# Moving the stores of a block-matching denoiser's two layers to later points of the issue order

## The chip, the cores and the metric

The kernel runs on 1 core of one Trainium2 chip. The metric is the time of one execution on the device in microseconds (us): before the change 6535.1 us, the median of three runs (6530.16 to 6537.6). A core has five engines that run side by side: TensorE (PE, with the loading of weights shown apart as PEld), VectorE (DVE), ScalarE (ACT), GpSimd (POOL) and SyncE (SP). Here POOL and SP issue nearly all DMA transfers, and each of them issues in order: an issue that must wait holds up everything behind it on its queue.

## The reference

`x` has 8 images of 32 channels and 128 x 128 pixels, in float32. Both layers begin with a group normalisation (16 groups of two channels) and end with a residual addition:

```
# layer 0: block matching, then a chain of convolutions
xn   = gn(x)
# for each pixel: the 8 of 25 offsets in a 5x5 window whose 3x3 patches differ least
xb   = the 8 shifted copies of xn -> 256 channels
dct  = grouped 1x1 (xb)
h    = relu(dw3x3(1x1(xb)));  h = relu(dw3x3(1x1(h)))
wien = sigmoid(dw3x3(1x1(h)))
x    = x + 1x1(grouped 1x1 (wien * dct))
# layer 1: one 5x5 filter, the same for all channels
x    = x + conv5x5(gn(x), pad=2)
```

## The kernel before, in words

**Slots.** An image is cut into 16 strips of 8 rows. The main loop has one step `s` for each strip, and one more per image (17 in all, `NS + 1`), and every step has four slots: `i = 3, 2, 1` for the three pairs of 1x1 and depthwise 3x3 convolution, each on a strip one step older than the last, and `i = 0` for the last product with `dct`. Half of the 256 channels go through the depthwise convolution on PE (`depthwise_t`, L751), the other half on VectorE (`depthwise_v`: one pass on ACT at L722, then eight of VectorE at L725 on a tile `tv`, then ACT at L729). Two rows of `tv` are carried to the next strip by a copy on SP's queue (`rows_before_v`, L655); the tiles `t` of PE's half are spread over the partitions by copies on SP's queue (L707, L709) and their last rows are carried by L648.

**Gathering.** Each slot also makes a quarter of the next strips' `xb`: POOL loads the index bytes (`gather_load`: `ib` at L602, three buffers, and pixels `xt` at L591), ACT makes selection masks from `ib` (L616, L617), and PE multiplies (L631). The search for the next image's offsets (`prep`, `squares` at L444, `costs`, whose sums are loaded into `dsum` at L492 and L499 and added on VectorE at L508 to L520, then the eight best of 25 at L536 and L537) is dealt out over the steps in small pieces.

**The residual.** `final_add` is a generator. For each strip PE makes the last 1x1 (`pa`, L831), and a resumption later VectorE adds it to the rows of `x` in `xr` (L839), takes their statistics (L840), and POOL stores the sum to the DRAM tile `x1d` in four transfers (L844). In the main loop `later` holds this generator. It is resumed twice in slot `i = 3`: ahead of the slot's product, and after `tick`.

**Layer 1.** After an image's last strip `layer1(b)` is pushed. It treats the channels eight at a time. For each such chunk (`c` = 0, 8, 16, 24) POOL loads `x1d` (L885 to L890), VectorE normalises (L897), PE makes the 5x5 filter as 40 matmuls with banded weights (L924), VectorE adds (L936), and POOL stores to `out` in four transfers (L938). The tiles `xy` and `xm` have two buffers each, and a chunk takes both. Rows 62 to 65 are not in those stores; `middle` makes them on VectorE with 25 passes (L972) and stores them at L981. Layer 1 of image b runs beside layer 0 of image b + 1; that of the last image runs alone at the end, with other buffers (`ends`, `xo`), all its chunks loaded at once, and the next chunk normalised ahead of the additions.

**The order.** Work that has no fixed place is a generator that yields the name of a queue ("D" for VectorE's pieces with a cost, "B", "A", "P", "Q") and optionally a number of turns to wait. `tick` (once per slot) or `turn` counts `now` up, runs pieces of "D" up to a credit and then "B"; the main loop runs "P", "Q" and "A" at fixed places of the slot, "A" after `tick`. PE, DVE and ACT keep the order in which the program issues (`ORDERED`, `manual_schedule`). POOL and SP are not among them: a planner sets their order by when it expects each transfer to be ready.

Of the kernel before, what the change touches and what calls it, by code (L numbers as in the profile page):

```python
# [44 lines left out]
def bm3d_conv_preact(  # L45
# [16 lines left out]
    nc = tc.nc  # L62
# [757 lines left out]
    def final_add(b, n, acc, xr, j0, j1):  # L820

        ya = R * n - 3 + j0
        whole = j1 - j0 == R
        nr, nw = (2, W) if whole else (j1 - j0, C)
        pa = ps_x.tile([P, 512], F32, name=f"pa_{b}_{n}", tag="x")
        pa = pa[:, : nr * nw].rearrange("p (r w) -> p r w", w=nw)
        for m in range(2):
            for j in range(4):
                ra = 2 * j if whole else j0
                xa = 0 if whole else C * j  # L830
                nc.tensor.matmul(  # L831
                    pa[C * j : C * (j + 1)],
                    lagg[:, m],
                    acc[m][:, ra : ra + nr, xa : xa + nw],
                    start=m == 0,
                    stop=m == 1,
                )
        yield
        nc.vector.tensor_add(xr, xr, pa)  # L839
        nc.vector.bn_stats(stats[b][:, n], xr)  # L840
        for j in range(4):
            ra = ya + 2 * j if whole else ya
            xa = 0 if whole else C * j
            nc.gpsimd.dma_start(  # L844
                x1d[b][:, ra : ra + nr, xa : xa + nw], xr[C * j : C * (j + 1)]
            )

    def layer1(b):

        yield "D", 0.2  # L850
        mv = work.tile([P, 2], F32, name=f"mv1_{b}", tag="mv1")
        nc.vector.bn_aggr(mv, stats[b].rearrange("p a b -> p (a b)"))
        mr = yield from group_stats(mv, f"b{b}")
        dg = work.tile([C, 2, C], F32, name=f"dg_{b}", tag="dg")
        for i in range(2):
            nc.vector.tensor_scalar(
                dg[:, i], ident[:C, :C], mr[:C, i : i + 1], None, op0=ALU.mult
            )
        yield "P", 0
        pb = ps_x.tile([P, 512], F32, name=f"pb_{b}", tag="x")  # L860
        nc.tensor.matmul(
            pb[:, : 2 * C], ones, dg.rearrange("p a b -> p (a b)"), start=True, stop=True
        )
        bc = work.tile([P, 2, C], F32, name=f"bc_{b}", tag="bc")
        nc.scalar.copy(bc.rearrange("p a b -> p (a b)"), pb[:, : 2 * C])
        last = b == NB - 1
        if last:
            ends = xnp.tile([P, HR, HX], F32, name="ends", tag="xn")
            ends = ends.rearrange("p r x -> p (r x)")[:, : 8 * 4 * W]
            ends = ends.rearrange("p (g c x) -> p g c x", g=8, x=W)  # L870
        xys = {}

        def load(c):


            if last:
                m = work.tile([P, 2, 4, W], F32, name=f"xo_{c}", tag="sel", bufs=4)
                t = [ends[:, c // 4], ends[:, c // 4 + 1], m[:, 0], m[:, 1]]
            else:
                t = [  # L880
                    work.tile([P, 4, W], F32, name=f"{name}_{b}_{c}_{e}", tag=name)
                    for name, e in (("xy", 0), ("xm", 0), ("xy", 1), ("xm", 1))
                ]
            src = x1d[b].rearrange("c y x -> y c x")
            nc.gpsimd.dma_start(t[0], src[:, c : c + 4])  # L885
            for h in range(2):
                nc.gpsimd.dma_start(
                    t[1][64 * h : 64 * h + 64], src[64 - 64 * h : P - 64 * h, c + 4 : c + 8]
                )
            nc.gpsimd.dma_start(t[2], src[:, c + 4 : c + 8])  # L890
            xys[c] = t

        def normalise(c):
            t = xys[c]
            for e in range(2):
                for i in range(4):
                    nc.vector.tensor_scalar(  # L897
                        t[3 - 2 * e][:, i],
                        t[e][:, i],
                        bc[:, 0, c + 4 * e + i : c + 4 * e + i + 1],  # L900
                        bc[:, 1, c + 4 * e + i : c + 4 * e + i + 1],
                        op0=ALU.subtract,
                        op1=ALU.mult,
                    )

        for c in range(0, C if last else 8, 8):
            load(c)
        push(middle(b, mr))
        for c in range(0, C, 8):
            if c == 0 or not last:  # L910
                yield "D", 2.0, 1 if last else 3
                normalise(c)
            yield "P", 0
            ps = [
                ps_x.tile([P, 4, W], F32, name=f"p5_{b}_{c}_{e}", tag="x") for e in range(2)
            ]
            t = xys.pop(c)

            for k, dx in enumerate((0, -2, -1, 1, 2)):
                xa, xz = max(0, -dx), min(W, W - dx)  # L920
                for h in range(2):
                    for e in range(2):
                        r, o = 64 * h, 64 * ((h + e) % 2)
                        nc.tensor.matmul(  # L924
                            ps[e][o : o + 64, :, xa:xz],
                            band[r : r + 64, dx + 2, r : r + 64],
                            t[3 - 2 * e][r : r + 64, :, xa + dx : xz + dx],
                            start=k == 0,
                            stop=k == 4,
                        )  # L930
            yield "D" if last else "B", 3.6 if last else 1.6
            if last and c + 8 < C:
                normalise(c + 8)
            for e in range(2):
                y = t[2 * e]
                nc.vector.tensor_add(y, y, ps[e])  # L936
                for a, z in ((0, 62), (66, P)):
                    nc.gpsimd.dma_start(  # L938
                        out[b, c + 4 * e : c + 4 * e + 4, a:z].rearrange("c y x -> y c x"),
                        y[a:z],  # L940
                    )
            if c + 8 < C and not last:
                yield "A", 0, 1
                load(c + 8)

        done.add((b, 0))
# [89 lines left out]
    with tc.manual_schedule(engines=ORDERED):  # L1036
# [17 lines left out]
        later = iter(())  # L1054

        for s in range(len(steps) + 2):
# [10 lines left out]
            for i in (3, 2, 1, 0):  # L1067
                si = s - (i - 1 if i else 2)
                live = 0 <= si < len(steps)
                new_v = new_t = iter(())  # L1070
                if live:
                    bi, ni = steps[si]

                if live and i:
                    src = source(i, bi, ni)
                    pointwise_v(i, bi, ni, lws[i - 1], src)
                    new_v, new_t = depthwise_v(i, bi, ni), depthwise_t(i, bi, ni)
                    accs[i, bi, ni] = [None, next(new_v)]
                next(later, None)
                if live and not i:  # L1080
                    if ni == 0:
                        x1d[bi] = dram.tile([C, H, W], F32, name=f"x1d_{bi}", tag="x1d")
                        stats[bi] = work.tile([P, NS + 1, 6], F32, name=f"stat_{bi}", tag="stat")
                    xr, xf, j0, j1 = fins.pop(si)
                run("P")
                if live and not i:
                    final_dct(bi, ni, accs[3, bi, ni], xf, j0, j1)

                run("Q")
                if s < len(steps):  # L1090
                    unit(gather_select, u + 1, (0,))
                    unit(gather_load, u + 3)
                    tick(b, i)
                next(later, None)
                next(new_v, None)
                if live and i:
                    pointwise_t(i, bi, ni, lws[i - 1], src)
                next(kept, None)
                if s < len(steps):
                    unit(gather_pixels, u)  # L1100
                next(dt, None)
                run("A")
                next(dv, None)
                if s < len(steps):
                    unit(gather_select, u + 1, (1,))
                    u += 1
                next(dt, None)
                kept, dv, dt = dv, new_v, new_t
                if live and not i:
                    later = end(bi, ni, xr, j0, j1)  # L1110
                if not i and 0 <= s - 1 < len(steps):
                    fins[s - 1] = final_load(*steps[s - 1])
# [66 lines left out]
```

## Time and profile before

| | |
|---|---|
| median of three runs | 6535.1 us |
| profiled execution, as timed | 6526.97 us |
| its span, first to last instruction | 6525.2 us |
| PE busy | 6180.3 us, 95% |
| DVE busy | 5856.5 us, 90% |
| ACT busy | 5051.0 us, 77% |
| POOL busy | 3077.3 us, 47% |
| granted TensorE clock, mean | 0.979 |
| an output store of layer 1 (L938, 124 KB), issue to landing | median 10.6 us |

The profile is one execution. A timeline line gives start and duration in us, engine, source line, operation, what is written from what, how many instructions are merged, and in brackets the idle time of the engine before it with what ended that. A line of the waits gives who waited, for whom, the us in total, the number of waits and the longest. "L725" is line 725 of the kernel. A wait is put down to what ended last by the profile.

### The profile page before, as it was taken

Reading aid. Unit: us, or ns where it says so; the run is one execution under the profiler, and the core shown is the slowest. Engines: PE = TensorE matmul, PEld = TensorE weight load, DVE = VectorE, ACT = ScalarE, POOL = GpSimd, SP = SyncE. Lnnn points to the kernel's source line nnn. Section 1 sums busy time; section 2 is a strip of 40 time slices with the busy share of each in tenths; the row PEclk is TensorE's granted clock in tenths of the full one; section 3 lists DMA queues with packets and bytes.
Section 4 is the critical chain, followed back from the end, with each engine's and each line's share of the span. In section 5 each row is a group of like instructions: output and inputs, shape, how many; then the busy total and the mean of one; then the engine's idle time right before and its main releaser. Section 6 shows DMA issues by size and latency. Waiting matters only on the chain.

```text
span 6525.2 us, 234180 instructions
## 1 busy us (share of the span) xinstructions
PE 6180.3 (95%) x102306; PEld 3262.3 (50%) x102306; DVE 5856.5 (90%) x8828; ACT 5051.0 (77%) x6698; POOL 3077.3 (47%) x5015
## 2 busy tenths in 40 slices
PE   5799999999999999999999999999999999999997
PEld 1445445544555546454555544544545454465553
DVE  7899988999889998899998999899998999988776
ACT  5787769778787877877778787887869787787772
POOL 8345436444364444643446534454345644344334
PEclk7899999999999999999999999999999999999998
DMA  4555555565555655655546556565555665455553
GB/s 85 125 135 144 123 124 146 145 143 135 133 145 139 142 147 127 150 140 135 141 129 157 140 131 151 127 150 137 139 134 138 150 147 133 118 149 147 137 135 79
DMA packets 544960, 886.21 MB, mean 136 GB/s; under 512 B 248880, under 2 KB 312944, under 8 KB 543936
## 3 DMA queue, kind: packets, MB, share of 16 engines
q0 software_dynamic: 383648, 611.87, 37.4%
q1 hardware_dynamic: 157776, 258.11, 16.4%
q8 instruction: 805, 13.19, 0.9%
q10 hardware_dynamic: 2512, 1.25, 0.1%
q14 instruction: 219, 1.79, 0.1%
HBM read 420.60 MB, written 216.49 MB: 98 GB/s over the span
## 4 chain that ended last, share of the span: by engine, by line
PE 50%; DVE 32%; ACT 5%; POOL 5%; DMA 4%; issue 4%; SPq 0%; ACTq 0%; DVEq 0%; POOLq 0%
DVE acc L725 21%; PE pw L751 16%; PE pv L670 12%; PE p L694 11%; PE pg L631 4%; DVE idx L537 3%; POOL xtd L424 3%; PE pc L810 2%; DVE df L444 2%; DVE acc L818 1%; PE p L924 1%; DVE mx L536 1%; PE pd L459 1%; DMA t<-t 1%; ACT sel L616 1%
## 5 line engine op out<-in xcount | busy, mean ns | idle before, releaser
L725 DVE SCALAR_TENSOR_TENSOR acc<-tv,dwv,acc 128x1024 f32<-128x1024 f32 (+3 forms) x3264 | 4031.6, 1237 | 156.3 <-ACT acc L722 52.0
L751 PE MATMUL pw<-t,dwd 96*32 96x254 f32 (+7 forms) x31680 | 2118.1, 419 | 23.0 <-DMA t<-t 10.1
L751 PEld LDWEIGHTS pw<-t,dwd 96*32 96x32 f32 (+1 forms) x31680 | 1105.7, 110 | 826.8 <-issue 369.3
L616 ACT ACTIVATE sel<-ib,nplace 128x1024 f32<-128x1024 uint8 x1024 | 1170.8, 1143 | 62.0 <-DMA ib<-idxd 62.0
L617 ACT ACTIVATE sel<-sel 128x1024 f32<-128x1024 f32 x1024 | 1086.0, 1061 | 32.5
L670 PE MATMUL pv<-acc,lw 128*32 128x512 f32 x8448 | 959.8, 590 | 54.4 <-DVE acc L818 47.8
L694 PE MATMUL p<-acc,lw 128*32 128x256 f32 x16768 | 974.3, 379 | 2.2 <-issue 2.2
L602 POOL DMA_DIRECT2D ib<-idxd x512 | 292.0, 570 | 1207.3 <-ACT sel L616 1078.1
L791 POOL DMA_DIRECT2D xf<-xbd x1088 | 651.0, 632 | 279.9 <-PE pc L810 180.6
L694 PEld LDWEIGHTS p<-acc,lw 128*32 128x32 f32 x16768 | 570.7, 111 | 393.6 <-issue 67.4
L729 ACT ACTIVATE acc<-acc 128x1024 f32<-128x1024 f32 (+3 forms) x408 | 417.1, 1022 | 390.2 <-DVE acc L725 389.8
L678 ACT COPY tv<-pv 128x512 f32<-128x512 f32 (+2 forms) x784 | 435.9, 579 | 338.5 <-PE pv L670 334.1
L631 PE MATMUL pg<-sel,xt 120*32 120x88 f32 (+1 forms) x24576 | 611.7, 244 | 64.8 <-ACT sel L617 56.1
L631 PEld LDWEIGHTS pg<-sel,xt 120*32 120x32 f32 x24576 | 559.5, 111 | 219.2 <-ACT sel L617 74.4
L670 PEld LDWEIGHTS pv<-acc,lw 128*32 128x32 f32 x8448 | 290.2, 110 | 532.3 <-issue 409.7
L764 ACT ACTIVATE acc<-pw 128x512 f32<-128x512 f32 (+2 forms) x808 | 436.6, 572 | 133.4 <-PE pw L751 131.8
L444 DVE TENSOR_TENSOR df<-xn 128x786 f32<-128x786 f32 (+2 forms) x576 | 530.4, 972 | 2.2 <-PE pd L459 1.9
L701 ACT COPY t<-p 128x512 f32<-128x512 f32 x800 | 421.7, 571 | 115.4 <-PE p L694 115.4
L452 ACT ACTIVATE df<-df 128x786 f32<-128x786 f32 (+2 forms) x576 | 458.9, 859 | 50.0 <-DVE df L444 48.6
L722 ACT ACTIVATE acc<-tv,dwv 128x1024 f32<-128x1024 f32 (+3 forms) x408 | 455.1, 1115 | 42.3 <-PE pa L831 24.8
L670 PE MATMUL pv<-xb,lw 128*32 128x512 f32 x4096 | 470.8, 596 | 0.0
L694 PE MATMUL p<-xb,lw 128*32 128x256 f32 x8192 | 469.9, 380 | 0.0
(155 smaller groups left out, 5893.0 us busy)
## 6 DMA issues: line engine op xcount, KB each, us to landing
ib<-idxd POOLq DMA_DIRECT2D x512, 256.0 KB, 4.0
xbd<-xb POOLq DMA_DIRECT2D x128, 1024.0 KB, 6.0
xf<-xbd POOLq DMA_DIRECT2D x960, 128.0 KB, 6.8
t<-t SPq DMA_DIRECT2D x792, 128.0 KB
t<-t SPq DMA_DIRECT2D x384, 256.0 KB
tv<-tv SPq DMA_DIRECT2D x384, 130.0 KB
xt<-xtd POOLq DMA_DIRECT2D x240, 180.0 KB, 4.0
xtd<-xl POOLq DMA_DIRECT2D x192, 96.0 KB, 3.3
```

The lines of the kernel that those rows point to most:

```text
L444: nc.vector.tensor_sub(df[:, :, ca:cz], xn[:, r0 : r0 + SR, ca:cz], xn[:, r0 + dy : r0 + dy + SR, ca + dx : cz + dx],)
L452: nc.scalar.activation(df[:, :, ca:cz], df[:, :, ca:cz], AF.Square)
L616: nc.scalar.activation(sel, ib, AF.Square, bias=nplace)
L617: nc.scalar.activation(sel, sel, AF.Relu, scale=-1.0, bias=1.0)
L631: nc.tensor.matmul(pg[C * j : C * (j + 1), :, :, xa:xz], xt[: 8 * QW, f * (NT // 2) + t], sels[j // 2][: 8 * QW, j % 2 * 2 : j % 2 * 2 + 2 ...
L670: nc.tensor.matmul(ps[C * j : C * (j + 1), :hr], lhsT[:, g, P + C * j : P + C * (j + 1)], src(g)[:, h : h + hr], start=g == 0, stop=g == 1,)
L694: nc.tensor.matmul(ps[C * r : C * (r + 1), e, :nb], lhsT[:, g, s], rows[:, r : r + 4 * nb - 3 : 4], start=g == 0, stop=g == 1,)
L722: nc.scalar.activation(acc, rows, AF.Copy, scale=tap)
L725: nc.vector.scalar_tensor_tensor(acc, rows, tap, acc, op0=ALU.mult, op1=ALU.add)
L751: nc.tensor.matmul(pt[u][C * j : C * (j + 1), ka:kz, :nb, xa:xz], dwd[0:hi, i - 1, u, j, dx + 1], t[0:hi, j, ka:kz, :nb, xa + dx : xz + dx ...
L764: nc.scalar.activation(rows[:, u : u + 2 * nh[u] - 1 : 2, :nb], pt[u][:, : nh[u], :nb], funcs[i - 1])
L791: nc.gpsimd.dma_start(xf[p : p + C, m, j0:j1], src[g, m, (h + m + 1) % 2, :, :, ya:yz])
```

## The change

Three edits, and no arithmetic is added or taken away.

- In `final_add` a `yield` stands between the statistics and the stores of the sum. The main loop resumes `later` a third time, at the end of the slot, so the stores are issued there.
- In `layer1` both additions of a chunk come first; then the task yields to queue "A" with one turn to wait, and the four output stores are issued when it is resumed.
- The yield ahead of the next chunk's loads is still there, so these come one more turn later, as does all that follows them. For the last image the first of these yields applies too.

```diff
@@ final_add
         yield
         nc.vector.tensor_add(xr, xr, pa)
         nc.vector.bn_stats(stats[b][:, n], xr)
+        yield
         for j in range(4):
             ra = ya + 2 * j if whole else ya
             xa = 0 if whole else C * j
@@ layer1
             for e in range(2):
-                y = t[2 * e]
-                nc.vector.tensor_add(y, y, ps[e])
+                nc.vector.tensor_add(t[2 * e], t[2 * e], ps[e])
+            yield "A", 0, 1
+            for e in range(2):
                 for a, z in ((0, 62), (66, P)):
                     nc.gpsimd.dma_start(
                         out[b, c + 4 * e : c + 4 * e + 4, a:z].rearrange("c y x -> y c x"),
-                        y[a:z],
+                        t[2 * e][a:z],
                     )
             if c + 8 < C and not last:
                 yield "A", 0, 1
@@ the main loop
                     unit(gather_select, u + 1, (1,))
                     u += 1
                 next(dt, None)
+                next(later, None)
                 kept, dv, dt = dv, new_v, new_t
                 if live and not i:
                     later = end(bi, ni, xr, j0, j1)
```

## The prediction

> **What bounds the kernel now.** I read the page's busy line and chain first, then the busy time by stretch of one image, then the waits, then the timelines of the places that the change touches. All times are of one profiled execution: span 6525.2 us, 6526.97 us as that run was timed, 8 us under the median of 6535.1 us. I make the sum against the 6525.2 us and add it to the median.
>
> ```profile
> span 6525.2 us, 234180 instructions
> PE 6180.3 (95%) x102306; PEld 3262.3 (50%) x102306; DVE 5856.5 (90%) x8828; ACT 5051.0 (77%) x6698; POOL 3077.3 (47%) x5015
> PE 50%; DVE 32%; ACT 5%; POOL 5%; DMA 4%; issue 4%; SPq 0%; ACTq 0%; DVEq 0%; POOLq 0%
> ```
>
> TensorE and VectorE pass the lead between them. The stretches (columns: window, us, busy time of PE, PEld, DVE, ACT, POOL, clock, DMA share, GB/s) are of image 2's pass, in which layer 1 of image 1 is also computed.
>
> ```profile
> 2060.00:2164.00 104.00, 103.32 (x1690) 53.78 (x1686) 93.62 (x127) 82.98 (x107) 53.30 (x86) 1.00 0.66 161
> 2164.00:2394.00 230.00, 223.31 (x3828) 114.17 (x3824) 220.81 (x378) 185.38 (x245) 95.95 (x164) 1.00 0.56 136
> ```
>
> Up to 2164 PE is busy for 103.3 of 104 us: PE sets the time. From 2164 to 2394 the roles are turned: VectorE has no recorded wait in this stretch, and PE waits for it.
>
> ```profile
> PE pv L670 <- DVE acc L818: 4.7, 3, 2.2
> ```
>
> In the waits of the whole run, the queue of POOL waits long for the two things that the change moves, and almost nobody waits for POOL:
>
> ```profile
> POOL x1d L844 <- DVE xr L839: 308.0, 60, 11.1
> POOL out_dram L938 <- DVE xy L936: 87.0, 22, 6.8
> ACT sel L616 <- DMA ib<-idxd: 62.0, 14, 10.3
> DVE xy L936 <- PE p L924: 39.9, 12, 7.6
> ```
>
> Columns: us in all, times, longest. The 62.0 us of late index loads are 52.8 us in seven waits of 5.5 to 10.3 us, each behind the 30 loads of L424 for the next image; the other seven share 9 us. So 395 us of POOL's waits are mostly cover. The fourth line is the one that counts: VectorE standing still for layer 1's matmuls. Six of its twelve waits are of the last chunk (4.4 to 7.6 us, 33.3 us together). Here is that of image 2:
>
> ```profile
> 2150.03 2.47 DVE L818 TENSOR_TENSOR acc<-acc,pc 128x512 f32<-128x512 f32 x4
> 2152.42 1.10 DVE L897 TENSOR_SCALAR xm<-xy,bc 128x128 f32<-128x128 f32 x4
> ...
> 2154.47 3.61 DVE L444 TENSOR_TENSOR df<-xn 128x780 f32<-128x780 f32 x4
> 2162.49 1.28 DVE L936 TENSOR_TENSOR xy<-xy,p 128x512 f32<-128x512 f32 x2 [4.41 <-PE p L924]
> 2163.69 0.41 DVE L839 TENSOR_TENSOR xr<-xr,pa 128x256 f32<-128x256 f32 x1
> 2164.49 10.52 DVE L725 SCALAR_TENSOR_TENSOR acc<-tv,dwv,acc 128x1024 f32<-128x1024 f32 x8
> ```
>
> **The change, part by part.** PE, DVE and ACT run in the order of the program; POOL and SP run in the order that the planner finds, so a line moved in the code need not move in the queue. I compared the built orders.
>
> *Stores of the sum (L844).* No arithmetic changes. For most slots POOL's order stays the same; moved are images' first and last slots and two of image 0. At the first slot the four stores go behind 13 loads of dsum (L492, L499). Before, the stores start at 1933.65 and dsum at 1938.51, so dsum comes up to 4.9 us earlier. VectorE's wait for it (4.1 us at 1951.0) shrinks, but 15 us later VectorE waits 1.5 us for PE, which was not waiting for VectorE; the gain turns into a longer wait there. Price 0, cover PE; without that cover up to 4.1 us per image.
>
> *Next loads and additions a turn later.* In six images the order on DVE and PE changes for chunks 16 and 24. Chunk 24's normalising goes behind L520, its 40 matmuls (4.4 us) with it, its additions behind the next L725 group. So at 2154.47 + 3.61 VectorE no longer waits for those matmuls but for pa (L831):
>
> ```profile
> 2156.97 1.06 PE L831 MATMUL pa<-acc,lagg 128*32 128x256 f32 x16
> 2157.96 4.48 PE L924 MATMUL p<-xm,band 64*64 64x512 f32 x40
> ```
>
> pa ends at 2158.03. From the residual's addition to L725 is 1.24 us where nothing is between (2112.14 to 2113.38, including a wait for ACT). L725 starts at about 2159.4 instead of 2164.49: 5.1 us. The moved work comes back inside the stretch that VectorE bounds: normalising 2.05 us (2152.42 to 2154.47), additions 1.2 us (2162.49 to 2163.69). Net 5.1 - 3.25 = 1.85 us, six times: 11 us gained. It isn't swallowed later, since PE waits for VectorE in this stretch. Chunk 16's additions now stand ahead of the residual's addition and make VectorE about 1 us later at 2114; the wait at 2158 still had 2 us, so this costs 0 as long as that remains.
>
> *SP's queue.* By the built orders one copy of tv (L655) moves ahead of a pair of copies of t (L707, L709) in each of these images. Before:
>
> ```profile
> 2126.92 0.46 SPq L707 DMA_DIRECT2D t<-t  x1
> 2127.44 1.03 SPq L709 DMA_DIRECT2D t<-t  x1
> 2130.72 0.46 SPq L648 DMA_DIRECT2D t<-t  x1
> 2133.96 0.48 SPq L655 DMA_DIRECT2D tv<-tv  x1
> ```
>
> The tv copy overwrites rows that the first five of eight L725 passes read, and that group begins at 2127.38: 5 x 1.31 = 6.6 us, so it can't go before 2133.9. The t pair, ready at 2126.9, and L648 now stand behind it until about 2134.4. The depthwise matmuls that need the pair begin at 2139.61, so 5.2 us are left; over the six images the tv copy stands 5.6 to 8.1 us ahead of them. From the DMA packets, a pair's 384 KB have moved a median 3.6 us after its issue (338 pairs with no output store issued near them), and 8.4 us with the stores in flight (37 pairs). So each image pays between 0 (3.6 under 5.2) and 3.2 us (8.4 - 5.2). After the change chunk 16's stores are issued there, behind additions at 2113 instead of 2108, and stretched because an issue of POOL waits for the landing of the eighth one before it (by the built order's semaphores; at 2119.92 a load waits 3.16 us for the store issued at 2108.40). I expect the last three issued between 2122 and 2126 and half landed by 2134. I take 1.0 us, nearer the low end: 6 us lost.
>
> *Output stores.* POOL's order puts one load of ib (of the 4-row strip 17, second half) and one of xt ahead of chunk 16's stores: better. Behind them stands ib for strip 18, whose select in ACT now starts 5.1 us after the landing in image 2 (2.2 us in the tightest image). I estimate its issue at 2136 to 2141 against 2136.78, so 0, with a bound of 3 us per image if the stores land at their slowest (14 us). Chunk 24's stores go behind two ib loads and ahead of an xf load; that load lands some 20 us before its use: 0.
>
> The Trainium skill, "DMA: Bandwidth & Descriptors", section "Anatomy of one DMA — SWDGE (gpsimd) path", gives 2.0 us plus bytes at 436 GB/s for such a DMA. By it, as an estimate, an output store of 124 KB lands in 2.3 us; its median here is 10.6 us. By the page the stores would be gone before the t pair is issued, the queue's price would be 0, and the whole change would gain 9 us; by the row it is what I have taken.
>
> *The end of the last image.* A chunk now takes two turns, so 25 passes of middle (0.39 us each) are dealt out otherwise: ten ahead of chunk 8's normalising, fifteen ahead of chunk 24's. All the work of VectorE remains. The last output store was issued at 6507.88; with chunk 8's additions 3 us later and chunk 24's matmuls behind 5.8 us more of middle, I get its issue at 6512.4, or 4.5 us later. But the 16 stores land one after the other about 2 us apart until 6523.12, and fewer are then in flight. Between 0 and 4.5 I take 2 us.
>
> Sum: -11 + 6 + 2 = -3 us, so 6532 us.
>
> **The rivals.**
> - *SP's queue decides (slower).* The t pair behind the tv copy meets the stores, and PE stands still. For: 8.4 us with stores in flight, against 5.2. Against: PE waits for t in only four places between 1000 and 6400, 5.8 us in all. Worst pair among the 37 is 10.4 us: 5.2 us per image, 31 us, less 11 and plus 2: +22 us, 6557 us. It decides "slower" from 3.7 us per image on.
> - *VectorE's wait goes for good (faster).* If the 3.25 us of moved work fall into a gap of VectorE, all 5.1 us remain: 31 us, less 6 for SP's queue and 2 for the end: -23 us, 6512 us. Against: no recorded wait of VectorE between 2164 and 2394. It decides "faster" from 3.5 us per image on.
> - *It doesn't do what it says.* The planner leaves most stores where they were, and what remains is the reordering of small pieces: 6535 us. This ends within 0.2%, as mine does.
>
> **How the numbers follow.** 0.2% is 13 us, about what a measurement of this kernel can tell. My forecast, with terms of -11 to 0, 0 to 19 and 0 to 4.5 us, has 0.47, the third rival 0.15: together 0.62 within 0.2%. VectorE's rival has 0.20. SP's has 0.18, the upper corner of my own terms included. The range leaves out the outer half of either outer rival: 6514 to 6552 us.
>
> **What would show it.** Right: DVE's waits for layer 1's matmuls (39.9 us) falling to some 10 us, L725 of that slot some 5 us earlier after pa, PE's waits for L818 a little less; POOL's waits for L839 and L936 changing with no answer in the span. SP: t pairs issued right after a tv copy in chunk 16's slot, and PE waits for t there of 0 to 3 us. The last store issued some 4 us later in the tail. Wrong: waits of PE for t, or of ACT for ib, of several us in every image; or an image's pass (788 us between first slots) changed by over 2 us.

## The result and the profile after

The change makes the kernel slower: 6548.3 us median (nine runs), against 6527.7 us of the kernel before in the same runs. The ratio is 1.0036, with a 95% interval of 1.0027 to 1.0044. The forecast was 6532 us and "within 0.2%"; the time lies inside the range of 6514 to 6552, but on the side that had 18 in 100. The profiled execution of the changed kernel took 6554.1 us (span 6552.3), 27.1 us more than that of before. It is the slowest of the nine; by the medians the loss is 20.6 us.

In the changed kernel lines behind the new `yield` have moved by one or two: the sum's stores are L845, layer 1's matmuls L925, the output stores L940. The page's busy line and chain:

```profile
span 6552.3 us, 234206 instructions
PE 6183.7 (94%) x102306; PEld 3242.6 (49%) x102306; DVE 5853.8 (89%) x8828; ACT 5055.7 (77%) x6698; POOL 3087.2 (47%) x5015
PE 48%; DVE 31%; POOL 6%; ACT 5%; DMA 5%; issue 4%; SPq 0%; ACTq 0%; DVEq 0%; POOLq 0%
```

PE's busy time is 3.4 us longer, DVE's 2.7 us shorter. PE stands idle 23.7 us longer (span less busy time), so most of the 27 us are waits. PE's waits between 1000 and 6400 us (columns: us in all, times, longest):

```profile
PE pv L670 <- DVE acc L818: 37.2, 21, 3.7
PE pd L459 <- ACT sm L470: 25.6, 6, 4.3
...
PE pw L751 <- DMA t<-t: 6.8, 4, 4.0
```

The first line fell from 45.2 us, as the prediction had hoped. The third, the price that I had feared, was 5.8 us before and hardly moved. The second line didn't exist before. `pd` is the PSUM tile in which the squared differences of a row group are summed; PE waits for ScalarE's copy of it to `sm` at L470, once in each of six images, 4.3 us each. Here is that of image 2's pass, first on PE, then on ScalarE:

```profile
2119.64 3.62 PE L670 MATMUL pv<-acc,lw 128*32 128x512 f32 x32
2123.07 0.84 PE L459 MATMUL pd<-df,neg 128*32 128x393 f32 x8
2128.18 1.55 PE L459 MATMUL pd<-df,neg 128*32 128x396 f32 x8 [4.26 <-ACT sm L470]
2129.50 5.95 PE L694 MATMUL p<-acc,lw 128*32 128x256 f32 x64
```

```profile
2120.37 3.11 ACT L452 ACTIVATE df<-df 128x786 f32<-128x786 f32 x4
2123.38 1.13 ACT L616 ACTIVATE sel<-ib,nplace 128x1024 f32<-128x1024 uint8 x1
2124.55 1.06 ACT L617 ACTIVATE sel<-sel 128x1024 f32<-128x1024 f32 x1
2125.51 1.05 ACT L678 COPY tv<-pv 128x512 f32<-128x512 f32 x2
2126.60 1.15 ACT L722 ACTIVATE acc<-tv,dwv 128x1024 f32<-128x1024 f32 x1
2127.66 0.47 ACT L470 COPY sm<-pd 128x396 f32<-128x396 f32 x1
```

The eight matmuls at 2123.07 are the last of row group 3, those at 2128.18 the first of group 4. (x8 counts records of the trace; a matmul of the program shows as two here, so these are four.) They stand directly behind one another. Before the change a slot lay between them. The pool of `pd` has one buffer (`ps_d`, `bufs=1`), so group 4 can't begin until ScalarE has copied group 3 out, and ScalarE does in order what stands ahead of the copy. PE keeps the program's order too, so all the work behind stands still with it: from 2123.94 to 2127.36 it executes nothing (first row of the table below).

Why do they stand together? The pieces of queue "D" are dealt out against a credit. Chunk 16's additions (queue "B") take 1.6 from it; now that they come a turn later, the turn that ends row group 3 begins with 3.05, by the kernel's own bookkeeping, where it had 1.45. Pieces are taken as long as credit is left. A pair costs 1.95, so 1.45 ended with the last pair of group 3, while 3.05 leaves 1.10 and takes the first pair of group 4 as well. On VectorE:

```profile
2110.34 3.64 DVE L444 TENSOR_TENSOR df<-xn 128x786 f32<-128x786 f32 x4
2114.47 1.28 DVE L936 TENSOR_TENSOR xy<-xy,p 128x512 f32<-128x512 f32 x2 [0.49 <-PE p L925]
```

Before, the additions came first (2107.43) and two L444 instructions behind them (2108.62); now there are four, and then the additions.

The stall isn't over at 2128.18. The columns of this view are window, us, busy time of PE, PEld, DVE, ACT, POOL, granted clock, DMA share, GB/s:

```profile
2123.94:2127.36 3.42, 0.00 (x0) 0.00 (x0) 3.35 (x4) 3.35 (x5) 1.50 (x2) 1.00 0.41 110
2127.36:2130.77 3.41, 2.60 (x20) 1.00 (x24) 3.38 (x4) 2.87 (x4) 3.41 (x3) 0.50 0.17 26
2130.77:2134.18 3.41, 3.41 (x36) 1.58 (x32) 3.30 (x4) 0.59 (x1) 0.82 (x2) 0.50 0.44 71
```

PE's granted clock is 0.50 behind the stall, and so the 64 matmuls of L694 take 5.95 us; the group of the same form at 2115.22 takes 3.66. Behind the six stalls these groups take 5.32, 5.95, 4.58, 5.30, 4.35 and 5.92 us instead of 3.64, and five of the six L459 groups ahead of them about 1.55 instead of 0.87: 9.6 and 3.4, together 13.0 us of slower clock. VectorE then waits for what PE delivers late (L722 stands behind two copies that wait for PE's L670), in place of the wait at L936 that the change removed here:

```profile
2146.86 10.53 DVE L725 SCALAR_TENSOR_TENSOR acc<-tv,dwv,acc 128x1024 f32<-128x1024 f32 x8 [5.91 <-ACT acc L722]
...
2168.31 0.42 DVE L839 TENSOR_TENSOR xr<-xr,pa 128x256 f32<-128x256 f32 x1 [4.99 <-PE pa L831]
```

The rest of the waits that the prediction spoke of, over the whole run:

```profile
POOL x1d L845 <- DVE xr L839: 311.8, 67, 10.5
POOL out_dram L940 <- DVE xy L936: 135.8, 13, 14.9
...
ACT sel L616 <- DMA ib<-idxd: 63.9, 12, 10.7
DVE xy L936 <- PE p L925: 41.5, 12, 9.5
```

POOL's waits for what the change moves grew by 53 us (308.0 and 87.0 before); e2 below moves the same stores and shows no loss. ScalarE's for the index loads stayed (62.0 before).

### The profile page after: what moved, and what is told of

Same layout as the page of the kernel before. It is cut to its first block, busy times and chain, and to the rows that moved or that the text cites. A ratio compares the mean times of both kernels' runs of the same rounds, so it can differ in the third digit from the quotient of the medians.

```text
span 6552.3 us, 234206 instructions
## 1 busy us (share of the span) xinstructions
PE 6183.7 (94%) x102306; PEld 3242.6 (49%) x102306; DVE 5853.8 (89%) x8828; ACT 5055.7 (77%) x6698; POOL 3087.2 (47%) x5015
## 4 chain that ended last, share of the span: by engine, by line
PE 48%; DVE 31%; POOL 6%; ACT 5%; DMA 5%; issue 4%; SPq 0%; ACTq 0%; DVEq 0%; POOLq 0%
DVE acc L725 20%; PE pw L751 16%; PE pv L670 12%; PE p L694 11%; PE pg L631 4%; DVE idx L537 3%; POOL xtd L424 3%; PE pc L810 2%; DVE df L444 2%; DVE acc L818 2%; PE pd L459 1%; DMA t<-t 1%; DVE mx L536 1%; ACT df L452 1%; PE p L925 1%
## 5 line engine op out<-in xcount | busy, mean ns | idle before, releaser
L616 ACT ACTIVATE sel<-ib,nplace 128x1024 f32<-128x1024 uint8 x1024 | 1170.7, 1143 | 64.1 <-DMA ib<-idxd 63.9
L670 PE MATMUL pv<-acc,lw 128*32 128x512 f32 x8448 | 963.0, 590 | 49.2 <-DVE acc L818 40.4
L694 PE MATMUL p<-acc,lw 128*32 128x256 f32 x16768 | 986.1, 383 | 2.6 <-DVE xy L936 2.6
L694 PEld LDWEIGHTS p<-acc,lw 128*32 128x32 f32 x16768 | 577.0, 112 | 398.4 <-issue 76.9
L670 PEld LDWEIGHTS pv<-acc,lw 128*32 128x32 f32 x8448 | 290.5, 110 | 528.8 <-issue 411.2
L444 DVE TENSOR_TENSOR df<-xn 128x786 f32<-128x786 f32 (+2 forms) x576 | 530.5, 973 | 1.0 <-PE pd L459 0.7
L452 ACT ACTIVATE df<-df 128x786 f32<-128x786 f32 (+2 forms) x576 | 457.6, 858 | 44.0 <-DVE df L444 43.0
L722 ACT ACTIVATE acc<-tv,dwv 128x1024 f32<-128x1024 f32 (+3 forms) x408 | 455.0, 1115 | 43.5 <-PE pa L831 27.4
L845 POOL DMA_DIRECT2D x1d<-xr x544 | 278.2, 517 | 409.7 <-DVE xr L839 311.8
L694 PE MATMUL p<-xb,lw 128*32 128x256 f32 x8192 | 468.7, 380 | 0.0
```

Of the source, the lines that this page charges most:

```text
L444: nc.vector.tensor_sub(df[:, :, ca:cz], xn[:, r0 : r0 + SR, ca:cz], xn[:, r0 + dy : r0 + dy + SR, ca + dx : cz + dx],)
L452: nc.scalar.activation(df[:, :, ca:cz], df[:, :, ca:cz], AF.Square)
L616: nc.scalar.activation(sel, ib, AF.Square, bias=nplace)
L670: nc.tensor.matmul(ps[C * j : C * (j + 1), :hr], lhsT[:, g, P + C * j : P + C * (j + 1)], src(g)[:, h : h + hr], start=g == 0, stop=g == 1,)
L694: nc.tensor.matmul(ps[C * r : C * (r + 1), e, :nb], lhsT[:, g, s], rows[:, r : r + 4 * nb - 3 : 4], start=g == 0, stop=g == 1,)
L722: nc.scalar.activation(acc, rows, AF.Copy, scale=tap)
```

## The experiments

Theory A: PE's new wait for the copy of `pd` is the loss. Rival B: the moved stores are the loss, on POOL or as transfers. Rival C: VectorE's pieces in their new places are the loss, and the wait only stands beside it. I call A1 and A2 two forms of A, below. All runs compute the whole result. Times are medians; each ratio is against runs of the kernel before on the same chip.

| run | us | before, us | ratio, 95% interval |
|---|---|---|---|
| the change | 6548.3 | 6527.7 | 1.0036 (1.0027 to 1.0044) |
| e1: sum's stores alone | 6533.4 | 6524.3 | 1.0011 (1.0002 to 1.0020) |
| e2: all stores, loads not | 6526.0 | 6524.4 | 1.0004 (0.9995 to 1.0013) |
| e3: loads later alone | 6538.1 | 6524.4 | 1.0027 (1.0018 to 1.0036) |
| e4: change, row groups kept apart | 6507.9 | 6524.4 | 0.9977 (0.9967 to 0.9986) |
| e5: before, squares a turn earlier | 6570.0 | 6524.4 | 1.0071 (1.0058 to 1.0085) |
| e6: change, two buffers for `pd` | 6912.9 | 6524.3 | 1.0599 (1.0585 to 1.0614) |
| e7: before, two buffers for `pd` | 6906.7 | 6524.3 | 1.0584 (1.0570 to 1.0599) |
| e9: e3, row groups kept apart | 6507.2 | 6524.3 | 0.9975 (0.9965 to 0.9986) |
| e10: change, first matmuls a turn later | 6509.0 | 6526.5 | 0.9973 (0.9962 to 0.9983) |
| e11: before, stall alone | 6536.2 | 6526.5 | 1.0018 (1.0009 to 1.0027) |
| e12: change, eight fillers | 6546.8 | 6526.5 | 1.0032 (1.0020 to 1.0044) |
| e13: change, four fillers | 6533.8 | 6525.5 | 1.0013 (1.0004 to 1.0023) |

Where I give times "by step", they are the stretches from one statistic of the residual (L840) to the next, compared with the trace of before and summed over images 1 to 6; the sixth step of an image ends at its sixth statistic.

### Which part of the change: e2, e3, e1

e2 is the change without the extra turn ahead of the loads:

```diff
             if c + 8 < C and not last:
-                yield "A", 0, 1
                 load(c + 8)
```

> The stores alone: the sum's stores at the end of their slot and the output stores a turn behind their additions, but the next chunk's loads in the same turn as before (only the extra turn ahead of them is taken out). The built order of TensorE and ScalarE is that of before, VectorE's differs only behind the last image. Theory A (what costs the time is TensorE's new wait for the copy of pd, L470, because the squares of the next row group come a turn earlier): no such wait here, so within 0.1% of before (0 to +2 us at the end, ratio 0.999 to 1.001). Rival B (the moved stores cost the time, on POOL or in the transfers): all of the +20 us of the whole change, ratio about 1.003. Rival C (VectorE's pieces in their new places cost it): as before, since they aren't moved.

Measured: 1.0004, no wait for the copy of `pd` between 1000 and 6400 us. Rival B falls: all the stores have moved and the loss isn't there.

e3 is the other half, the kernel before with one number changed:

```diff
             if c + 8 < C and not last:
-                yield "A", 0, 1
+                yield "A", 0, 2
                 load(c + 8)
```

> The next loads a turn later alone: all stores where they were, one more turn ahead of the next chunk's loads. The built orders of TensorE, VectorE and ScalarE are those of the changed kernel up to the last image's end. Theory A: the wait for the copy of pd comes back, six times 4.3 us, less the gain at the last chunk's matmuls: +15 to +22 us, ratio about 1.003. Rival B (stores): 0, ratio 1.000. Rival C (VectorE's pieces): as A, but without the wait for pd in the trace.

Measured: 1.0027, +13.7 us, just under the 15 to 22 us that A expected. The wait is back in PE's list, with the same sum as in the changed kernel:

```profile
PE pv L670 <- DVE acc L818: 41.7, 20, 3.6
PE pg L631 <- ACT sel L617: 39.2, 24, 2.2
PE pd L459 <- ACT sm L470: 25.6, 6, 4.3
```

So the loss comes with the loads' extra turn. Whether it is the wait (A) or the pieces' places (C) this run can't say. It is not quite the other half: in its trace VectorE normalises chunk 24 (L897) ahead of the additions of `dsum` (L508 to L520), in the changed kernel behind them.

e1 has the third resumption of `later` and the `yield` in `final_add`, and nothing else:

```diff
         nc.vector.bn_stats(stats[b][:, n], xr)
+        yield
...
                 next(dt, None)
+                next(later, None)
```

> The stores of the sum at the end of their slot, alone. TensorE, VectorE and ScalarE keep the order of before. My forecast priced this part at 0. In the changed kernel and in the run with the stores alone TensorE waits 3 to 5 us more at L810 in the images' second step (rows there: ScalarE's copy L701, loads of xf). If the sum's stores push the loads of xf behind them, this shows here: 0 to +5 us and those waits; if it is the output stores, 0 and waits as before (9.9 us and none for xf).

Measured: 1.0011, +9 us, more than I expected. PE's waits at L810 for ScalarE's row rose from 9.9 to 13.9 us, and 1.0 us for xf is new. They are 13.1 to 14.3 us in all the runs with these stores moved (e2, e4, e10, e12, e13) and 9.0 to 10.4 us in those without (e3, e9, e11): some 4 us come from the sum's stores. That isn't 9, though, and e2 holds the same edit and lost 1.6 us; the intervals of the two overlap (1.0002 to 1.0013). The part's price is small and not settled: between 0 and some 9 us.

### The wait itself: e4, e10, e5, e11

e4 is the change with a rule more in the queue: the first pair of a row group (`FIRST`) isn't taken in a turn that took a pair already.

```diff
-    PAIR = 1.95
+    PAIR, FIRST = 1.95, 1.9501
...
-                    if at <= now[0] and (c != PAIR or pairs[0] < limit)
+                    if at <= now[0]
+                    and (c != PAIR or pairs[0] < limit)
+                    and (c != FIRST or pairs[0] < min(limit, 1))
...
-            pairs[0] += cost == PAIR
+            pairs[0] += cost in (PAIR, FIRST)
...
-                yield "D", PAIR
+                yield "D", FIRST if b and aa[0] == 2 else PAIR
```

> The whole change, with one rule more: the first pair of squares of a row group isn't taken in the same turn as the last pair of the group ahead of it. Then the first matmuls of pd_4 stand a slot behind the copy of pd_3 again, as before the change, while chunks 16 and 24 stay a turn later. Theory A: TensorE's wait for the copy of pd (25.6 us in the changed kernel) is gone, and with it the loss: 6548 - 22 = about 6526 us, ratio to before 0.998 to 1.001. Rivals B and C: as the changed kernel, ratio about 1.003.

Measured: 0.9977, 6507.9 us. The wait is gone and the loss with it, and more: 40 us below the changed kernel (37 when each is set against its own runs of before). Theory A had put 22 us on it, since the recorded wait is only 25.6 us. So a stall costs some 6 to 7 us, not 4.3. There are two readings. A1: the stall costs more than its own length, through the clock behind it. A2: taking the squares a turn early costs something on ScalarE and VectorE as well (L452 has four instructions ahead of the copy, not two). In e4 both are undone.

e10 separates them. The squares stay early; only the first matmuls of group 4 are held back:

```diff
-        yield "Q", 0
+        if b > 1 and i == 4 and aa[0] == 2:
+            yield "Q", 0, 1
+        else:
+            yield "Q", 0
```

> The changed kernel, with only the first matmuls of row group 4 held back by one turn; the squares stay a turn early on VectorE and ScalarE, whose orders are the changed kernel's. Theory A1 (TensorE's standing still is the cost, 4.26 us of wait and the slower clock behind it, about 6.6 us each): no wait for the copy L470, and 6548 - 40 = about 6508 us, ratio 0.997 to 0.9985. Theory A2 (the squares' early place on ScalarE and VectorE has a price of its own, up to the 14 us by which the loss exceeds the recorded wait): 6520 to 6525 us, ratio 0.9995 to 1.000.

Measured: 0.9973, 6509.0 us, what A1 expected. The squares' early place costs nothing; A2 falls, and with it C, since VectorE and ScalarE keep the changed kernel's order to the last instruction. On PE the first matmuls of group 4 now stand one slot later, merged with the next pair into 16, and nothing waits:

```profile
2109.48 0.83 PE L462 MATMUL pd<-df,neg 128*32 128x390 f32 x8
2110.13 3.63 PE L697 MATMUL p<-acc,lw 128*32 128x256 f32 x64
...
2123.13 1.52 PE L462 MATMUL pd<-df,neg 128*32 128x396 f32 x16
```

L697 here is the group that is L694 in the changed kernel: 3.63 us, not 5.95.

e5 puts the stall into the kernel before, by way of the squares:

```diff
-                yield "D", PAIR
+                if not (b and b < 7 and i == 4 and aa[0] == 2):
+                    yield "D", PAIR
+                if b and b < 7 and i == 4 and aa[0] == 0:
+                    yield "D", PAIR
                 push(squares(b, i, pd, xn, aa, sq, idx))
```

> The kernel before, with only the first pair of squares of row group 4 taken a turn earlier in images 1 to 6 (the credit that it costs is charged a turn later, so that all else keeps its place). Theory A: the wait for the copy of pd appears six times at about 4.3 us: +20 to +26 us, ratio 1.003 to 1.004. Rivals B and C: 0, ratio 1.000.

Measured: 1.0071, +45.6 us, twice what A expected. An image's squares are made in the pass of the image before, so this caught passes 0 to 5, and not 1 to 6 as in the changed kernel. In pass 0 the wait is longer. Over the whole run:

```profile
PE pd L462 <- ACT sm L473: 31.6, 7, 6.9
```

By step, passes 1 to 5 lost 27.3 us at the place, 5.5 each, and pass 0 lost 8.8 us: 36.1 of the 36.8 us by which this profiled execution is longer. (The median lost 9 us more; that part has no trace.) The sign is as expected; the price per stall is again above its length.

e11 puts a stall into the kernel before without moving a square. The last matmuls of group 2 are held back until they stand directly ahead of group 3's:

```diff
-        yield "Q", 0
+        if b > 1 and i == 2 and aa[0] == 5:
+            yield "Q", 0, 2
+        else:
+            yield "Q", 0
```

> The kernel before, with the last matmuls of row group 2 held back by two turns in the same six passes, so that they stand directly ahead of the first matmuls of group 3. No square, no addition and no store moves; only those matmuls and the copy of their result. Theory A1: TensorE waits for the copy six times, 2.5 to 4.3 us each by the work that ScalarE has ahead of it (two selections, two copies, L722), and its clock falls to half behind the longer ones: +15 to +40 us, ratio 1.002 to 1.006. Theory A2: 0, ratio 1.000.

Measured: 1.0018, +9.7 us, below the 15 us that A1 expected, and not A2's 0. The stalls are shorter here:

```profile
1973.61 0.83 PE L462 MATMUL pd<-df,neg 128*32 128x393 f32 x8
1977.23 0.87 PE L462 MATMUL pd<-df,neg 128*32 128x396 f32 x8 [2.79 <-ACT sm L473]
1977.92 3.64 PE L697 MATMUL p<-acc,lw 128*32 128x256 f32 x64
```

The clock did not fall here (3.64 us for L697). It didn't behind three of the six stalls; behind the other three it did (4.61, 4.61 and 4.33 us). Yet 9.7 us is less than the 16.7 us of the recorded waits alone: about 1.6 us for each stall (1 to 3 by the interval). The place explains it in part. In image 2 VectorE has no recorded wait in the step with the stall, before or now, and the step takes as long as before:

```profile
1967.90:2014.75 46.85, 46.65 (x848) 25.61 (x844) 45.19 (x83) 37.28 (x49) 20.41 (x31) 1.00 0.53 133
```

```profile
1967.52:2014.36 46.84, 44.05 (x768) 22.65 (x764) 45.18 (x84) 35.30 (x46) 22.68 (x35) 1.00 0.53 136
```

The first row is the kernel before, the second e11. What PE left undone it does in the next step, which is 2.2 us longer. Over the six images these two steps lost 8.9 us. So a stall has no fixed price: it depends on the clock behind it and on what the other engines have to do at the place.

### The clock behind the stall: e12, e13

If the clock is the missing part, work for PE in the stall must bring it back. Ahead of the first matmuls of group 4 I put matmuls into a PSUM tile that nobody reads:

```diff
         yield "Q", 0
+        if b > 1 and i == 4 and aa[0] == 2:
+            pz = ps_x.tile([P, 512], F32, name=f"pz_{b}", tag="x")
+            for _ in range(8):
+                nc.tensor.matmul(
+                    pz[:, :496], ident, cst[:, :496], start=True, stop=True
+                )
```

> The changed kernel with eight matmuls of 128 x 496, whose result nobody reads, between the last matmuls of pd_3 and the first of pd_4 (some 3.5 us of TensorE's work in a stall of 4.26 us; computes nothing). If the granted clock falls because TensorE stands still, it stays at 1.00 here, the matmuls of L694 behind the stall take 3.6 us instead of 5.95, and 6 x 2.3 = 14 us come back: about 6534 us, ratio 1.001 to 1.002. If the clock has another cause, as the changed kernel: ratio 1.0036.

Measured: 1.0032, no gain. My estimate of the fillers' length was wrong: they take 6.92 us, not 3.5.

```profile
2120.40 0.83 PE L465 MATMUL pd<-df,neg 128*32 128x390 f32 x8
2121.16 6.92 PE L457 MATMUL pz<-cst 128*128 128x496 f32 x16
2128.01 0.87 PE L465 MATMUL pd<-df,neg 128*32 128x396 f32 x8
2128.70 3.64 PE L700 MATMUL p<-acc,lw 128*32 128x256 f32 x64
```

From pd_3 to pd_4 it is 7.6 us, against 5.1 in the changed kernel: 2.5 us lost. L700 (that is L694) takes 3.64 and L465 0.87: 3.0 us won. The 2.5 us are lost six times, 15 us, against the 13.0 us of slower clock that are gone. So the time hid the answer, and the row gave it. e13 has `range(4)` in place of `range(8)`.

> The run with the filler again, with four such matmuls instead of eight (the eight took 6.92 us, 0.43 us for each of 16 passes, so they outlasted the stall of 4.26 us by what the clock gave back; four are 3.46 us). If the clock's fall behind the stall is part of the price: clock 1.00, L694 behind it 3.6 us instead of 5.95, and 6 x 2.3 = 14 us come back against the changed kernel: about 6534 us, ratio 1.001 to 1.002. If the loss of clock is made up elsewhere: ratio 1.003 to 1.004.

Measured: 6533.8 us, 1.0013, where 6534 was expected. Here the fillers end before the copy does:

```profile
2115.24 3.59 PE L457 MATMUL pz<-cst 128*128 128x496 f32 x8
2119.60 0.87 PE L465 MATMUL pd<-df,neg 128*32 128x396 f32 x8 [0.76 <-ACT sm L476]
2120.29 3.64 PE L700 MATMUL p<-acc,lw 128*32 128x256 f32 x64
```

```profile
2119.60:2124.00 4.40, 4.40 (x87) 2.62 (x91) 4.32 (x4) 2.65 (x4) 3.36 (x3) 1.00 0.27 35
```

The clock stays at 1.00 (L700 takes 3.64 us behind all six), and 12 to 14 us are back, though PE reaches the first matmuls of group 4 no earlier than in the changed kernel: 5.1 us behind the last of group 3 in both. Now the bill closes: 25.6 us of waits and 13.0 us of slower clock are 38.6 us, and the sixth steps of the changed kernel are together 38.0 us longer than those of e10. The medians are 39 us apart, or 38 when each is set against its own runs of before.

### Left over: e6 and e7, e9

Giving `pd` a second buffer takes the stall away without moving anything. PSUM is full, so the pool of the other tiles falls from five to four; e7 is the control.

```diff
-        tc.tile_pool(name="ps_x", bufs=5, space=bass.MemoryType.PSUM)
+        tc.tile_pool(name="ps_x", bufs=4, space=bass.MemoryType.PSUM)
...
-        tc.tile_pool(name="ps_d", bufs=1, space=bass.MemoryType.PSUM)
+        tc.tile_pool(name="ps_d", bufs=2, space=bass.MemoryType.PSUM)
```

> The changed kernel with two buffers for pd and four instead of five for the other tiles in PSUM; the order of TensorE, VectorE and ScalarE is the changed kernel's. To be read against the next run, which has the same pools without the change. Theory A1 (TensorE stands still because pd has a single buffer): no wait for the copy L470, and this run is 0 to 17 us faster than the next one. Theory A2 (the wait is only a sign, and the squares a turn earlier cost the time on ScalarE and VectorE whatever the buffer): 10 to 20 us slower than the next one.

> The kernel before with two buffers for pd and four for the other tiles in PSUM: the control for the run ahead. Before has no wait for the copy of pd, so the second buffer gains nothing, and one buffer fewer can cost: 0 to +60 us against before.

Measured: both are some 380 us slower than before, six times what I allowed for, and the change is 6 us slower than its control (the intervals overlap), between what A1 and A2 expected. PE waits for VectorE now:

```profile
PE pg L631 <- DVE acc L818: 322.7, 85, 11.6
```

The pair isn't conclusive as a whole, since another wait bounds it. At the disputed place it agrees with A1: the sixth and seventh steps of the images (where the stall was) are together 24 us shorter than in the control, about what they are in e4.

e9 asks whether a version with the later loads but without the moved stores is better still. It is e3 with the rule of e4.

> All stores where they were, only the next loads a turn later, and the rule that keeps a row group's first squares out of the turn of the last ones. If the moved stores cost about 7 us of the changed kernel (it lost 20.6 us, the later loads alone 13.7), this is 7 us faster than the whole change with the rule: 6524 - 24 = 6500 us, ratio 0.996 to 0.997. If that difference is chance, 6508 us, ratio 0.9977.

Measured: 6507.2 us, 0.9975. It equals e4 and e10 within their intervals (some 6 us); the moved stores neither cost nor gain more than that there. All three beat both kernels: the one before by some 17 us, the changed one by some 40. e10 needs the smallest edit.

## Why the prediction was wrong

- **The step that failed** is "Next loads and additions a turn later". It says "In six images the order on DVE and PE changes for chunks 16 and 24", and prices those moves alone. The built orders show more: a pair of squares (L444) moves a turn forward in the same six images, and its matmuls (L459) land directly behind the last of the former row group. I gave that no price. It cost 25.6 us of waits and 13.0 us of slower clock, some 38 us in all.
- **The gain in the same step** was right in kind and too small. With the stall taken away (e10), the sixth steps are 44.3 us shorter and the seventh 21.9 us longer: 7.4 us gained and 3.65 us returned per image, against 5.1 and 3.25 in the prediction. That is 22 us, not 11. The 5.1 us were worked out for image 2 and taken six times. Its step came out 5.5 us shorter, but its wait of 4.41 us was among the shortest; in image 3, where VectorE had waited 7.57 us, the step is 10.5 us shorter.
- **SP's queue**, +6 us, and the rival built on it: the reordering came, the cost didn't. In the changed kernel's chunk 16 slot the pair of `t` follows a tv copy as expected:

```profile
2135.29 0.48 SPq L655 DMA_DIRECT2D tv<-tv  x1
2136.14 1.91 SPq L707 DMA_DIRECT2D t<-t  x1
2138.10 1.45 SPq L709 DMA_DIRECT2D t<-t  x1
```

  PE's waits for t went from 5.8 to 6.8 us in all, and none of the four falls into an image's sixth step. In the traces this order comes only in kernels with the stall at that place (the change, e3, e5, e12); in e4, e9, e10 and e13 the pair goes ahead of the tv copy, as before. So no run has the reordering without the stall; that it costs nothing is read from PE's waits.
- **Output stores at 0**: ScalarE's waits for `ib` went from 62.0 to 63.9 us, so this came. The 10.6 us for a store (table and prediction) is too low, though: that median is of all stores to `out`, the 32 small ones of `middle` (16 KB) among them. L938 alone has 11.4 us, 8.6 to 16.6, so 14 us was not the slowest.
- **The sum's stores at 0**: the exchange of waits came as written. In image 2 VectorE's wait for `dsum` fell from 4.1 to 1.9 us, and the wait at L936 behind it grew from 1.5 to 5.2 us (at 1970.0). The price isn't quite 0: some 4 us at L810, and as told above not settled up to 9.
- **The tail**, +2 us: the stretch from the last statistic to the end is 0.5 us longer, inside the bounds of 0 to 4.5.
- **What I said would show it**: the wait at L936 for the last chunk is gone in all six images, but the sum of such waits didn't fall to 10 us (39.9 to 41.5), because the first chunk's grew, to 2.8 to 6.8 us an image. I had seen that exchange in one place and forgotten it in the other.
- **The rivals**: "VectorE's wait goes for good", 6512 us, asked for a net gain of over 3.5 us per image. Without the stall it is 3.7 us, and e10 stands at 6509. The rival that ended slower named the wrong mechanism: the sign came from PE's `pd`, not from SP. That the time lies inside the range is luck, since the upper part of the range was made for SP's queue.

## What to carry to other kernels

When a change shifts a piece of work that is dealt out against a budget, list every instruction that the new order moves on each engine, not only those that the change names; another piece takes the freed place. Look there for two groups on a tile with a single buffer that have become neighbours, and read what the engine that empties the tile has ahead of the copy: that is the stall. Price a stall of TensorE with the clock behind it, ask whether another engine covers it at that place, and try first to move the second group by a turn, which here turned a loss of 0.36% into a gain of 0.27%.

## What I hadn't expected of the hardware

- A stall of 4.26 to 4.29 us cost TensorE another 1.4 to 3.0 us (13.0 us over the six): behind it the granted clock was 0.50 (rows of 2127.36 and 2130.77), and with matmuls in the stall it was 1.00. In the trace of the changed kernel the stretches of low clock are 3.41 us long or a multiple, at 0.50, and all their starts and ends lie on one grid of 3.413 us (the last is cut off by the end). The Trainium skill, "TensorE: Matmul & The Clock Gate", section "Part 1: The HAM clock gate (the 'warmup' mystery)", tells of a free-running window of 3413 ns and half the clock after an idle one; length and grid agree.
- A window need not be idle, and shorter waits can do it too. The same page, section "Why this matters for your kernels", advises against idle gaps over about 3 us. In the changed kernel two waits of 2.2 us were followed by different clocks. Here are the windows of the grid around them:

```profile
3530.24:3533.65 3.41, 1.19 (x26) 0.61 (x24) 2.63 (x4) 3.38 (x5) 2.05 (x4) 1.00 1.02 203
3533.65:3537.06 3.41, 3.41 (x66) 3.21 (x62) 3.31 (x5) 3.13 (x5) 2.02 (x4) 0.50 0.39 132
```

```profile
3093.33:3096.74 3.41, 1.80 (x36) 0.77 (x28) 3.34 (x4) 0.03 (x1) 2.74 (x6) 1.00 0.94 329
3096.74:3100.16 3.42, 2.84 (x28) 0.94 (x32) 3.32 (x13) 3.39 (x4) 0.58 (x1) 1.00 1.07 263
```

  The first wait lies inside one window, and PE is busy for 35% of it; the second is shared by two windows, with 53% and 83%. Counted over all 14 traces (1000 to 6400 us, PE's busy time by its records): of the windows at full clock, half the clock followed all 313 in which PE was busy for under 40%, 65 of 343 with 40 to 60%, and none of some 20,900 above. Of the windows at half the clock, full clock followed none of 145 under 75%, 22 of 42 with 75 to 90%, and all 356 above. So the measurement is stricter than the page, and it decides: what counted was how much of a window was filled. It fits e11 too: its three stalls with a fall left a window filled to 22, 21 and 38%, the other three were shared by two windows of 45 to 74%.
- The eight matmuls of 128 x 496 with 128 columns of weights show as 16 records of 0.43 us each (6.92 us together), while the 32 records of L670, of 128 x 512 with 32 columns, take 3.62 us together.
